# A four-layer graph network on one core: layer 3's gates and layer 1's update computed with features on partitions, and layer 0's identity added to the adjacency in place

## The chip, the core and the metric

The kernel runs on one core of a Trainium2 chip. A core has TensorE (PE: matrix products, and transposes, into PSUM), VectorE (DVE), ScalarE (ACT), GpSimd (POOL) and SyncE (SP, which here issues nearly all DMAs). The metric is the device time of one execution in microseconds (us), lower is better.

## What is computed

There are 32 independent graphs (batches `b`) of 512 nodes with 128 features each, and a dense 512 x 512 adjacency per graph. Everything is float32. Each layer normalises its input `x`, applies a relu, runs a graph layer on it and adds the result to `x`. Cut to what matters:

```python
# layer 0
adj = adj + eye; r = sum(adj, -1) ** -0.5
x = x + leaky_relu((adj * r[:, :, None] * r[:, None, :]) @ (h @ W) + b)
# layer 1
in_rep, out_rep, node_rep = elu(h @ W_in.T + b_in), elu(h @ W_out.T + b_out), elu(h @ W_node.T + b_node)
upd = concat([adj @ in_rep, node_rep, adj.T @ out_rep])
x = x + tanh(upd @ W_upd.T + b_upd)
# layer 2: four sub-layers with l2-normalised adj and adj.T
# layer 3 (a GRU cell)
m = tanh(adj @ (h @ W_msg.T + b_msg))
r = sigmoid(m @ Wih_r + h @ Whh_r + b_r); z = sigmoid(m @ Wih_z + h @ Whh_z + b_z)
n = tanh(m @ Wih_n + bih_n + r * (h @ Whh_n + bhh_n))
x = x + (1 - z) * n + z * h
```

## The kernel before

**Two layouts.** A tile of one graph is 128 partitions x 512 values. In "rows" the nodes lie on partitions (four chunks of 128 nodes, 128 features each); in "features" (names ending in T, and `f`, `agg`, `y` of layer 2) the features lie on partitions and the 512 nodes along the row. The residual `x` and the normalisation live in rows, since the moments of a node are then taken along a partition. Products with the adjacency take rows as the stationary operand and give features. So the stages turn between the layouts. `turned` (L645) does it without PE: a DVE transpose of 32 x 32 blocks into `blk` (L649), four DMAs of 64 KB into a DRAM buffer (L658), one DMA of 256 KB back (L662), and a copy or an addition that reads the result in another order of columns (`turned_cols`). In batches 0, 1 and 31 (`at_ends`) four PE transposes do it instead (L677, L800, L1069).

**The order.** `program(b)` records the operations of each batch with an engine, an estimated cost and what they read and write. `Plan.order` (L173) then runs a list scheduler over all of them: an operation's key is its batch's due time (`PERIOD` per batch, `ENDING` for the last) less the length of the chain behind it, and buffers come from counted pools (`bank` 8 PSUM banks, `s2` tiles of 2 KB per partition, `s4`, `s8` for adjacency). The order that comes out is the static order of each engine's queue. Loads marked `yields` are planned only while no turn is under way (`plan.way`). `kept_warm` (L257) writes filling products (`ps_idle`, L1137) where the plan has PE idle for more than 0.7 us. Two to three batches are in work at a time.

**What the change touches.**
- Layer 0, L923 and after: `diag` gets the four diagonal blocks of `aT` plus the identity (`own`, one DVE addition into a tile of its own). The sum over neighbours then takes for each of four chunks the diagonal block from `diag` and the rest from `aT`, ten products of 128 to 384 columns into `ps_agg`.
- Layer 1's update: `linear_rows` (L696) with the node data as the stationary operand, twelve products of 128 columns that give rows; then the bias `u1` (DVE, L981), tanh (ACT, L983) and the addition to `x1` (DVE, L985).
- Layer 2 starts from `x2`: moments (L586, L588, L589), a power on POOL (L628), `nb` (L636), four ACT operations for `h` (L640), a turn, the copy `f0` (ACT, L682), and the first product `ps_sd<-w_sb,f`.
- Layer 3: `seven("gates", ...)` (L720) computes the 2 x 2 block product of the r and z gates, for nodes in two halves, with seven products instead of eight; each is two products of 128 columns (L759) that give rows. Eight more of 128 columns make the n gate. Biases are added on DVE (`gn`, L1109), then two tanh (L1115), `u`, `n`, `q`, `w`, and `xo` (L1131), which is stored. The last batch goes another way (`gates_turned`, L503).

Of the kernel before, what the change touches and what calls it, by code (L numbers as in the profile page):

```python
# [14 lines left out]
AF = mybir.ActivationFunctionType  # L15
# [9 lines left out]
PERIOD = 35.0  # L25
ENDING = 1.5
SMALL = 8
OWN = 32
# [4 lines left out]
SEVEN = {"last": 0 * 5 * D, "gates": 1 * 5 * D}  # L33
FIFTEEN = 5 * D * len(SEVEN)
# [3 lines left out]
RING = {"inv": 4, "invT": 4}  # L38
# [32 lines left out]
C_COLS = C_L3 + 6  # L71
# [3 lines left out]
R_L0, R_L1_IO, R_L1_UPD, R_L3_MSG, R_L3_G, R_L3_HRZ = (k * D for k in (0, 1, 3, 4, 5, 9))  # L75
R_COLS = 9 * D
# [205 lines left out]
def gnn_stack(  # L282
# [16 lines left out]
    plan = Plan(sb, psum, {"bank": 8, "s2": 39, "s4": 5, "s8": 9}, {"bank": 0, "s2": 5, "s4": 0, "s8": 0})  # L299
# [19 lines left out]
    def t_mm(n):  # L319
        return n * 0.00166 + 0.0085  # L320
# [35 lines left out]
    def blocks(site):  # L356


        if site == "gates":
            return [c + k * D for c in (W_L3_HH, W_L3_IH) for k in range(2)], W3, (r_sb, R_L3_G), (RS, {2})  # L360
        return [W_L2[3][0] + (2 * k + o) * D for k in (2, 0) for o in range(2)], (W2F, {3}), (rf_sb, ROW_OF[3] * 2 * D), RF
# [10 lines left out]
    def setup():  # L372
# [6 lines left out]
        def spread(lo, hi, to=None):  # L379
            return lambda: nc.sync.dma_start(  # L380
                r_sb[:, lo:hi] if to is None else to.ap()[:, :hi - lo], bass.AP(tensor=brow.tensor, offset=brow.offset + lo, ap=[[0, P], [1, hi - lo]]))
# [9 lines left out]
        hrz = plan.buf("s2", (P, N), "hrz")  # L391
        op("SP", 0.5, spread(R_L3_HRZ, R_L3_HRZ + 2 * D, hrz), [], [hrz], kb=D)
        op("DVE", 0.4, lambda: nc.vector.tensor_add(r_sb[:, R_L3_G:R_L3_G + 2 * D], r_sb[:, R_L3_G:R_L3_G + 2 * D], hrz.ap()[:, :2 * D]),
           [(RS, {2}), hrz], [(RS, {2})])
# [50 lines left out]
        for site, at in SEVEN.items():  # L445
            (b11, b12, b21, b22), wbuf, (bias, c), bbuf = blocks(site)
# [11 lines left out]
            combine(4, lambda o, m=bias, c=c: nc.vector.tensor_sub(o, m[:, c:c + D], m[:, c + D:c + 2 * D]), [bbuf])  # L458
# [33 lines left out]
    def program(b):  # L492
# [8 lines left out]
        rows_shape = (P, NC, D)  # L501

# [142 lines left out]
        def turned(m, name):  # L645
# [17 lines left out]
            plan.way(m.uses[0][0], back)  # L663
            return mT

# [54 lines left out]
        def seven(site, x1, x2, dst, part, behind):  # L720

            at = SEVEN[site]
            (b11, b12, b21, b22), wbuf, (bias, bc), bbuf = blocks(site)
# [179 lines left out]
        def tt(dst, fn, n, reads, engine="DVE"):  # L905
            return op(engine, t_tt(n), fn, reads, [dst])

# [12 lines left out]
        def own(k, n):  # L920
            t = aT.ap()
            blocks = bass.AP(tensor=t.tensor, offset=t.offset + k * (N + P), ap=[list(t.ap[0]), [N + P, n], [1, P]])
            own_engine.tensor_tensor(diag.ap()[:, k:k + n, :], blocks, ident[:, None, :].to_broadcast([P, n, P]), op=ALU.add)  # L923

        n = NC if b else 1
        own_engine, own_name = (nc.vector, "DVE") if b < OWN else (nc.gpsimd, "POOL")
        for k in range(0, NC, n):
            op(own_name, t_tt(n * P) if b < OWN else t_pool(n * P), lambda k=k, n=n: own(k, n), [(aT, set(range(k, k + n))), ID], [(diag, set(range(k, k + n)))])
        psh = plan.bank("agg")
        for c in range(NC):  # L930
            for lo, hi in ((0, c * P), (c * P, (c + 1) * P), ((c + 1) * P, N)):
                if lo == hi:
# [3 lines left out]
                   hi - lo, c == 0 and lo == 0, c == NC - 1 and hi == N, [(hr, {c}), (diag if lo == c * P else aT, {c})])  # L936
        agg = buf("s2", name="agg")
# [25 lines left out]
        for h in range(2):  # L963
# [15 lines left out]
        linear_rows(psu, [W_L1_UPD, W_L1_UPD + D, W_L1_UPD + 2 * D], [agg_in, node, agg_out], (W1, {1}))  # L979
        u1, y1 = buf("s2", name="u1"), buf("s2", name="y1")  # L980
        tt(u1, lambda: nc.vector.tensor_add(u1.ap().rearrange("p (c v) -> p c v", c=NC), psu.ap().rearrange("p (c v) -> p c v", c=NC),  # L981
                                            along(r_sb, R_L1_UPD, D, NC)), N, [psu, (RS, {1})])
        op("ACT", t_act(N), lambda: nc.scalar.activation(y1.ap(), u1.ap(), AF.Tanh), [u1], [y1])  # L983
        x2 = buf("s2", rows_shape, "xr")
        tt(x2, lambda: nc.vector.tensor_add(flat(x2), flat(x1), y1.ap()), N, [x1, y1])  # L985
# [43 lines left out]
        for i, (wsd, wn) in enumerate(W_L2):  # L1029
# [8 lines left out]
            if i == 3:  # L1038
                sd = buf("s4", (P, NC, 2 * D), "sd")
                seven("last", f0, f, *of_halves(sd), [third_started])  # L1040
            else:
                sd = paired_rows([f], wsd, (W2F, {i}), rf_sb, RF, ROW_OF[i] * 2 * D)
# [22 lines left out]
        x3 = buf("s2", rows_shape, "xr")  # L1065
        if at_ends:
            pst = plan.bank("t")
            for c in range(NC):
                op("PE", 0.109, lambda c=c: nc.tensor.transpose(pst.ap()[:, c * P:(c + 1) * P], f.ap()[:, c * P:(c + 1) * P], ident),  # L1069
                   [f, ID], [(pst, {c})])  # L1070
            tt(x3, lambda: nc.vector.tensor_add(flat(x3), flat(x2), pst.ap()), N, [x2, pst])
        else:
            f4 = turned(f, "f4r")
# [114 lines left out]
```

## Time and profile before

| what | value |
|---|---|
| median of 4 runs | 2276.22 us (2275.66 to 2276.32) |
| the profiled execution | 2275.91 us, of it 2274.1 in the span of the profile |
| PE matmul instructions | 9328, two for each product, one for each transpose |
| `ps_agg<-a,sd`, 128x512 | x768, 593 ns each by the profile |
| `ps_seven<-t_sb,s`, 128x128 | x756, 275 ns each |
| turns: `turned<-turn_turned`, 256 KB | x116, 2.6 us from issue to landing |
| `turn_turned<-blk`, 64 KB | x464, 1.8 us |
| all DMA queues | q1: 231.29 MB, 32.7% of 16 engines |
| granted PE clock | 1.0 |

A line of a profile's group names the line of the code, the engine, the operation, out<-in by the program's names, shape and count. A wait names who waited and for whom, then the sum in us, how often, and the longest. L353 is the helper through which most products pass, so the names tell more there than the line does.

### The profile page before, as it was taken

What the parts mean: (1) busy time and instruction counts of PE and PEld (TensorE: products, weight loads), DVE (VectorE), ACT (ScalarE), POOL (GpSimd) and SP (SyncE); (2) the same over time, 40 slices, a digit from 0 to 9 for tenths busy, and PEclk for the clock granted to TensorE, in tenths of its full rate; (3) what the DMA queues carried; (4) which work ended last, traced back from release to release, by engine and by line L of the source; (5) the groups of instructions that cost most, each with busy time, mean ns of one, the idle gap of its engine ahead of it and who ended that gap; (6) DMA issues with size and microseconds to landing.
All of it is one profiled execution on the core that took longest, in us unless ns stands there. A gap on an engine that the chain in (4) does not pass through costs nothing.

```text
span 2274.1 us, 28426 instructions
## 1 busy us (share of the span) xinstructions
PE 2267.1 (100%) x9328; PEld 1447.3 (64%) x9328; DVE 1660.8 (73%) x4539; ACT 1016.8 (45%) x2408; POOL 225.9 (10%) x203
## 2 busy tenths in 40 slices
PE   9999999999999999999999999999999999999999
PEld 7666666666566665666666666656666666666666
DVE  7757677777777786777776777767778677777666
ACT  7644344543445533445434455334454344552222
POOL 2100011100011100111000110101110001100000
PEclk9999999999999999999999999999999999999999
DMA  7122333333323333233333333332333323332111
GB/s 281 38 84 76 122 90 107 107 104 121 114 86 107 102 114 119 84 106 102 118 116 94 106 112 98 116 121 81 106 102 116 121 87 111 101 103 77 56 42 51
DMA packets 157444, 233.24 MB, mean 103 GB/s; under 512 B 21360, under 2 KB 96368, under 8 KB 157296
## 3 DMA queue, kind: packets, MB, share of 16 engines
q1 hardware_dynamic: 157008, 231.29, 32.7%
q8 instruction: 74, 1.21, 0.2%
q14 instruction: 74, 0.61, 0.1%
q10 hardware_dynamic: 288, 0.13, 0.0%
HBM read 184.43 MB, written 46.92 MB: 102 GB/s over the span
## 4 chain that ended last, share of the span: by engine, by line
PE 97%; DMA 1%; DVE 1%; ACT 0%; POOL 0%; SPq 0%; issue 0%; ACTq 0%; DVEq 0%
PE ps_agg L353 62%; PE ps_fifteen L838 9%; PE ps_seven L759 9%; PE ps_sd L353 7%; PE ps_upd L353 4%; PE ps_gate L353 3%; PE ps_msg L353 1%; PE ps_lin L353 1%; PE ps_node L353 1%; DMA raw<-in_raw 0%; DMA bounce<-invT 0%; DMA hrz<-in_brow 0%; DMA a<-in_adj 0%; POOL sc L628 0%; DMA turn_turned<-blk 0%; PE ps_t L677 0%
## 5 line engine op out<-in xcount | busy, mean ns | idle before, releaser
L353 PE MATMUL ps_agg<-a,sd 128*128 128x512 f32 x768 | 390.8, 593 | 0.0
L353 PE MATMUL ps_agg<-aT,sd 128*128 128x512 f32 x768 | 372.7, 593 | 0.1
L628 POOL TENSOR_TENSOR sc<-v,neg_half 128x4 f32<-128x4 f32 (+1 forms) x127 | 165.9, 1307 | 1764.7 <-DVE v L589 1165.3
L353 PEld LDWEIGHTS ps_agg<-aT,sd 128*128 128x128 f32 x768 | 137.7, 191 | 104.3 <-issue 98.5
L640 ACT ACTIVATE h<-xr,nb,sc 128x128 f32<-128x128 f32 x384 | 164.3, 485 | 51.6 <-DVE nb L636 50.2
L353 PEld LDWEIGHTS ps_agg<-a,sd 128*128 128x128 f32 x768 | 132.2, 191 | 69.0 <-issue 65.5
L912 ACT ACTIVATE sq<-a 128x512 f32<-128x512 f32 x124 | 78.2, 631 | 202.3 <-DMA a<-in_adj 201.4
L759 PEld LDWEIGHTS ps_seven<-t_sb,s 128*128 128x128 f32 x756 | 111.9, 191 | 46.7 <-issue 37.1
L353 PE MATMUL ps_sd<-w_sb,f 128*128 128x256 f32 x512 | 138.7, 380 | 0.0
L353 PE MATMUL ps_agg<-aT,f1r 128*128 128x512 f32 x256 | 131.0, 593 | 0.1
L353 PE MATMUL ps_agg<-f,w_sb 128*128 128x512 f32 x256 | 130.9, 593 | 0.1
L353 PE MATMUL ps_agg<-aT,rep 128*128 128x512 f32 x256 | 130.7, 593 | 0.1
L353 PE MATMUL ps_agg<-a,rep 128*128 128x512 f32 x256 | 130.7, 592 | 0.0
L353 PE MATMUL ps_agg<-a,f1r 128*128 128x512 f32 x256 | 130.7, 592 | 0.0
L353 PE MATMUL ps_agg<-aT,msg 128*128 128x512 f32 (+1 forms) x264 | 130.0, 580 | 0.0
L353 PEld LDWEIGHTS ps_sd<-w_sb,f 128*128 128x128 f32 x512 | 92.5, 190 | 54.3 <-issue 36.1
L965 ACT ACTIVATE rep<-sd 128x512 f32<-128x512 f32 x64 | 40.1, 628 | 187.4 <-PE ps_agg L353 179.6
L759 PE MATMUL ps_seven<-t_sb,s 128*128 128x128 f32 x756 | 120.0, 275 | 0.0
L1018 DVE TENSOR_TENSOR a<-a,rows 128x512 f32<-128x512 f32 x128 | 87.5, 686 | 42.5 <-PE ps_agg L353 42.1
L715 DVE TENSOR_TENSOR sd<-ps_sd,r_sb 128x512 f32<-128x512 f32 x64 | 44.0, 687 | 98.0 <-PE ps_sd L353 98.0
L715 DVE TENSOR_TENSOR sd<-ps_sd,rf_sb 128x512 f32<-128x512 f32 x128 | 85.8, 671 | 33.3 <-PE ps_sd L353 32.3
L649 DVE STREAM_TRANSPOSE blk<-h 128x512 f32<-128x512 f32 x87 | 61.4, 705 | 60.9 <-ACT h L640 60.9
(224 smaller groups left out, 4673.7 us busy)
## 6 DMA issues: line engine op xcount, KB each, us to landing
aT<-in_adjt SPq DMA_DIRECT2D x124, 512.0 KB, 6.4
a<-in_adj SPq DMA_DIRECT2D x62, 512.0 KB, 5.9
turn_turned<-blk SPq DMA_DIRECT2D x464, 64.0 KB, 1.8
turned<-turn_turned SPq DMA_DIRECT2D x116, 256.0 KB, 2.6
rows<-bounce SPq DMA_DIRECT2D x32, 512.0 KB, 4.0
shares<-bounce SPq DMA_DIRECT2D x32, 512.0 KB, 4.3
x<-in_x SPq DMA_DIRECT2D x32, 256.0 KB, 10.4
out<-xo SPq DMA_DIRECT2D x31, 256.0 KB
```

The lines of the kernel that those rows point to most:

```text
L353: op("PE", t_mm(n), lambda: nc.tensor.matmul(out_of(ps.ap()), lhs(), rhs(), start=start, stop=stop), reads, [ps], later=later)
L628: op("POOL", t_pow(n), lambda: nc.gpsimd.tensor_tensor(inv.ap()[:, :n], v8.ap()[:, :n], neg_half[:, :n], op=ALU.pow), [v8, NH], [(inv, {0})])
L640: op("ACT", t_act(D, 2), lambda c=c: nc.scalar.activation(h.ap()[:, c, :], xin.ap()[:, c, :], AF.Relu, bias=nb.ap()[:, c:c + 1], scale=inv ...
L649: op("DVE", t_tt(N), lambda: nc.vector.transpose(blk.ap().rearrange("p b (c r) -> p c b r", c=NC), m.ap().rearrange("p c (b s) -> p c b s" ...
L715: op("DVE", t_tt(N), lambda ps=ps, h=h: nc.vector.tensor_add(sd.ap()[:, 2 * h:2 * h + 2, :], ps.ap().rearrange("p (j v) -> p j v", j=2), a ...
L759: op("PE", t_mm(D), lambda j=j: nc.tensor.matmul(ps.ap()[:, k * H + j * D:k * H + (j + 1) * D], lhs()[:, j * P:(j + 1) * P], rhs(), start= ...
L838: op("PE", t_mm(H), lambda: nc.tensor.matmul(o[0](), weight(), data[0](), start=first, stop=True, skip_group_check=True), [data[1], wbuf], ...
L912: op("ACT", 0.73, lambda c=c: nc.scalar.activation(sq.ap(), a.ap()[:, c, :], AF.Copy, accum_out=sums.ap()[:, c:c + 1]), [(a, {c})], [sq, ( ...
L965: op("ACT", t_act(N), lambda s=s: nc.scalar.activation(rep.ap()[:, s, :], io.ap()[:, s, :], AF.Exp), [(io, halves)], [(rep, part)])
L1018: op("DVE", t_tt(N), lambda m=m, c=c, s=s: nc.vector.tensor_mul(m.ap()[:, c, :], m.ap()[:, c, :], rows.ap()[:, s, :]), [(m, {c}), rows], [ ...
```

## The change

Layer 3's gates (all batches but the last) are computed with features on partitions: a new function `gates` runs the seven block products with weights as the stationary operand and 256 nodes as moving columns, adds bias and scale in the activations, and gives the cell's output `y` as features. Layer 1's update uses `linear_t` (weights stationary, three products of 512 columns), with the bias in the tanh. Both results are turned back to rows and added to `x` by a new function `added_rows`, which uses `turned`, or PE transposes in batches 0, 1 and 31. In layer 0 (all batches but the first) ACT saves the diagonal blocks of `aT` in `diag`, DVE adds the identity to them in place, four products of 512 columns run over `aT`, and ACT copies the blocks back. The constants of the plan change with it: the cost of a product, `PERIOD`, `ENDING`, the pools, and 16 DRAM buffers for turns instead of 8. The rows of biases for the old gates and the update, with their loads, are gone.

```diff
--- before.py
+++ after.py
-PERIOD = 35.0
-ENDING = 1.5
+PERIOD = 37.0
+ENDING = -3.5
...
-SEVEN = {"last": 0 * 5 * D, "gates": 1 * 5 * D}
-FIFTEEN = 5 * D * len(SEVEN)
+GATES = 5 * D
+FIFTEEN = GATES + 4 * D
...
-RING = {"inv": 4, "invT": 4}
+RING = {"inv": 4, "invT": 4, "turn_turned": 16}
...
-    plan = Plan(sb, psum, {"bank": 8, "s2": 39, "s4": 5, "s8": 9}, {"bank": 0, "s2": 5, "s4": 0, "s8": 0})
+    plan = Plan(sb, psum, {"bank": 8, "s2": 36, "s4": 5, "s8": 10}, {"bank": 0, "s2": 4, "s4": 0, "s8": 0})
...
-        return n * 0.00166 + 0.0085
+        return n * 0.00166 + (0.0123 if n <= P else 0.0094)
...
+        def gates(h3T, mT):
+
+
+            H = N // 2
+            (b11, _, b21, b22), bank = BOTH, {}
+            s12, s34 = (buf("s2", name=k) for k in ("s12", "s34"))
+            hn, r, z, p1, d, n, y, w = (buf("s2", name=k) for k in ("hn", "r", "z", "p1", "d", "n", "y", "w"))
+
+            def half(m, k):
+                return (lambda: m.ap()[:, k * H:(k + 1) * H]), (m, {k})
+
+            def bank_half(name, k):
+                ps = bank[name]
+                return (lambda: ps.ap()[:, k * H:(k + 1) * H]), ps
+
+            def dve(o, x, y, sub=False):
+                op("DVE", t_tt(H), lambda: nc.vector.tensor_tensor(o[0](), x[0](), y[0](), op=ALU.subtract if sub else ALU.add), [x[1], y[1]], [o[1]])
+
+            def product(o, data, weight, wbuf, first):
+                op("PE", t_mm(H), lambda: nc.tensor.matmul(o[0](), weight(), data[0](), start=first, stop=True, skip_group_check=True), [data[1], wbuf], [o[1]])
+
+            def plain(col):
+                return lambda: wt(col), W3
+
+            def made(k):
+                return lambda: t_sb[:, GATES + k * D:GATES + (k + 1) * D], (TS, {GATES + k})
+
+            h0, h1, m0, m1 = half(h3T, 0), half(h3T, 1), half(mT, 0), half(mT, 1)
+            s1, s2, s3, s4 = half(s12, 0), half(s12, 1), half(s34, 0), half(s34, 1)
+            dve(s3, h0, h1, True)
+            bank["n"] = plan.bank("gate")
+            mm(bank["n"], lambda t: t, lambda: wt(W_L3_HH + 2 * D), h3T.ap, N, True, True, [h3T, W3])
+            op("ACT", t_act(N, 1), lambda: nc.scalar.activation(hn.ap(), bank["n"].ap(), AF.Identity, bias=cg_sb[:, 2:3], scale=0.5), [bank["n"], CG], [hn])
+            dve(s1, h1, m1)
+            dve(s2, s1, h0, True)
+            dve(s4, m0, s2, True)
+            for k in "abc":
+                bank[k] = plan.bank("seven")
+            A, Bc, C = bank_half("a", 0), bank_half("b", 0), bank_half("c", 0)
+            P1, D1, E1 = half(p1, 0), half(d, 0), half(d, 1)
+            product(A, h0, *plain(b11), True)
+            op("ACT", t_act(H), lambda: nc.scalar.copy(P1[0](), A[0]()), [A[1]], [P1[1]])
+            product(Bc, s2, *made(1), True)
+            product(C, s1, *made(0), True)
+            dve(D1, Bc, P1)
+            product(A, m0, *plain(b21), False)
+            op("ACT", t_act(H, 1), lambda: nc.scalar.activation(half(r, 0)[0](), A[0](), AF.Tanh, bias=cg_sb[:, 0:1], scale=0.5), [A[1], CG], [(r, {0})])
+            product(Bc, s3, *made(2), False)
+            dve(E1, Bc, P1)
+            dve(half(z, 1), C, E1)
+            product(Bc, m1, *made(3), False)
+            dve(half(r, 1), Bc, P1)
+            op("ACT", t_act(H, 1), lambda: nc.scalar.activation(half(r, 1)[0](), half(r, 1)[0](), AF.Tanh, bias=cg_sb[:, 0:1], scale=0.5), [(r, {1}), CG], [(r, {1})])
+            product(C, s4, *plain(b22), False)
+            dve(half(z, 0), C, D1)
+            op("ACT", t_act(N, 1), lambda: nc.scalar.activation(z.ap(), z.ap(), AF.Tanh, bias=cg_sb[:, 1:2], scale=0.5), [z, CG], [z])
+            bank["i"] = plan.bank("gate")
+            mm(bank["i"], lambda t: t, lambda: wt(W_L3_IH + 2 * D), mT.ap, N, True, True, [mT, W3])
+            tt(hn, lambda: nc.vector.scalar_tensor_tensor(hn.ap(), r.ap(), 1.0, hn.ap(), op0=ALU.add, op1=ALU.mult), N, [r, hn])
+            tt(n, lambda: nc.vector.tensor_add(n.ap(), hn.ap(), bank["i"].ap()), N, [hn, bank["i"]])
+            op("ACT", t_act(N, 1), lambda: nc.scalar.activation(n.ap(), n.ap(), AF.Tanh, bias=cg_sb[:, 3:4]), [n, CG], [n])
+            tt(w, lambda: nc.vector.tensor_sub(w.ap(), h3T.ap(), n.ap()), N, [h3T, n])
+            tt(w, lambda: nc.vector.scalar_tensor_tensor(w.ap(), z.ap(), 1.0, w.ap(), op0=ALU.add, op1=ALU.mult), N, [z, w])
+            tt(y, lambda: nc.vector.scalar_tensor_tensor(y.ap(), w.ap(), 0.5, n.ap(), op0=ALU.mult, op1=ALU.add), N, [w, n])
+            return y
...
-        def turned(m, name):
+        def turned(m, name, quiet=False):
...
-            plan.way(m.uses[0][0], back)
+            if not quiet:
+                plan.way(m.uses[0][0], back)
             return mT
+
+        def added_rows(x, m, quiet=False):
+
+            o = buf("s2", rows_shape, "xr")
+            if at_ends:
+                ps = plan.bank("t")
+                for c in range(NC):
+                    op("PE", 0.109, lambda c=c: nc.tensor.transpose(ps.ap()[:, c * P:(c + 1) * P], m.ap()[:, c * P:(c + 1) * P], ident),
+                       [m, ID], [(ps, {c})])
+                tt(o, lambda: nc.vector.tensor_add(flat(o), ps.ap(), flat(x)), N, [x, ps])
+            else:
+                t = turned(m, "last" if quiet else "turned", quiet)
+                tt(o, lambda: nc.vector.tensor_add(o.ap().rearrange("p c (a r) -> p c a r", a=NC), turned_cols(t), x.ap().rearrange("p c (a r) -> p c a r", a=NC)),
+                   N, [x, t])
+            return o
...
         def own(k, n):
             t = aT.ap()
             blocks = bass.AP(tensor=t.tensor, offset=t.offset + k * (N + P), ap=[list(t.ap[0]), [N + P, n], [1, P]])
-            own_engine.tensor_tensor(diag.ap()[:, k:k + n, :], blocks, ident[:, None, :].to_broadcast([P, n, P]), op=ALU.add)
-
-        n = NC if b else 1
-        own_engine, own_name = (nc.vector, "DVE") if b < OWN else (nc.gpsimd, "POOL")
-        for k in range(0, NC, n):
-            op(own_name, t_tt(n * P) if b < OWN else t_pool(n * P), lambda k=k, n=n: own(k, n), [(aT, set(range(k, k + n))), ID], [(diag, set(range(k, k + n)))])
+            return blocks, ident[:, None, :].to_broadcast([P, n, P])
+
+        def own_blocks():
+            return own(0, NC)[0]
+
+        if b:
+            op("ACT", t_act(N), lambda: nc.scalar.copy(diag.ap(), own_blocks()), [aT], [diag])
+            op("DVE", t_tt(N), lambda: nc.vector.tensor_tensor(own_blocks(), diag.ap(), own(0, NC)[1], op=ALU.add), [diag, ID], [aT])
+        else:
+            for k in range(NC):
+                op("DVE", t_tt(P), lambda k=k: nc.vector.tensor_tensor(diag.ap()[:, k:k + 1, :], *own(k, 1), op=ALU.add), [(aT, {k}), ID], [(diag, {k})])
         psh = plan.bank("agg")
-        for c in range(NC):
+        for c in range(NC if b == 0 else 0):
             for lo, hi in ((0, c * P), (c * P, (c + 1) * P), ((c + 1) * P, N)):
                 if lo == hi:
                     continue
                 mm(psh, lambda t, lo=lo, hi=hi: t[:, lo:hi], lambda c=c: hr.ap()[:, c, :],
                    (lambda c=c: diag.ap()[:, c, :]) if lo == c * P else (lambda c=c, lo=lo, hi=hi: aT.ap()[:, c, lo:hi]),
                    hi - lo, c == 0 and lo == 0, c == NC - 1 and hi == N, [(hr, {c}), (diag if lo == c * P else aT, {c})])
+        if b:
+            aggregate(psh, hr, 0, aT)
+            op("ACT", t_act(N), lambda: nc.scalar.copy(own_blocks(), diag.ap()), [diag], [aT])
         agg = buf("s2", name="agg")
...
-        linear_rows(psu, [W_L1_UPD, W_L1_UPD + D, W_L1_UPD + 2 * D], [agg_in, node, agg_out], (W1, {1}))
-        u1, y1 = buf("s2", name="u1"), buf("s2", name="y1")
-        tt(u1, lambda: nc.vector.tensor_add(u1.ap().rearrange("p (c v) -> p c v", c=NC), psu.ap().rearrange("p (c v) -> p c v", c=NC),
-                                            along(r_sb, R_L1_UPD, D, NC)), N, [psu, (RS, {1})])
-        op("ACT", t_act(N), lambda: nc.scalar.activation(y1.ap(), u1.ap(), AF.Tanh), [u1], [y1])
-        x2 = buf("s2", rows_shape, "xr")
-        tt(x2, lambda: nc.vector.tensor_add(flat(x2), flat(x1), y1.ap()), N, [x1, y1])
+        linear_t(psu, [W_L1_UPD, W_L1_UPD + D, W_L1_UPD + 2 * D], [agg_in, node, agg_out], (W1, {1}))
+        y1 = buf("s2", name="y1")
+        op("ACT", t_act(N, 1), lambda: nc.scalar.activation(y1.ap(), psu.ap(), AF.Tanh, bias=c_sb[:, C_L1_UPD:C_L1_UPD + 1]), [psu, CS], [y1])
+        x2 = added_rows(x1, y1)
...
-        x3 = buf("s2", rows_shape, "xr")
-        if at_ends:
-            pst = plan.bank("t")
-            for c in range(NC):
-                op("PE", 0.109, lambda c=c: nc.tensor.transpose(pst.ap()[:, c * P:(c + 1) * P], f.ap()[:, c * P:(c + 1) * P], ident),
-                   [f, ID], [(pst, {c})])
-            tt(x3, lambda: nc.vector.tensor_add(flat(x3), flat(x2), pst.ap()), N, [x2, pst])
-        else:
-            f4 = turned(f, "f4r")
-            tt(x3, lambda: nc.vector.tensor_add(
-                x3.ap().rearrange("p c (a r) -> p c a r", a=NC), x2.ap().rearrange("p c (a r) -> p c a r", a=NC), turned_cols(f4)),
-               N, [x2, f4])
+        x3 = added_rows(x2, f)
...
-        seven("gates", h3T, mT, lambda k, o: g.ap()[:, 2 * k:2 * k + 2, o * D:(o + 1) * D],
-              lambda k, o: (g, fields((2 * k, 2 * k + 1), (o,))), [messages])
...
-        u, n, q, w, xo = (buf("s2", rows_shape, k) for k in ("u", "n", "q", "w", "xo"))
-        tt(u, lambda: nc.vector.scalar_tensor_tensor(u.ap(), gate(0), 1.0, gate(3), op0=ALU.add, op1=ALU.mult), N, [column(0), column(3)])
-        tt(u, lambda: nc.vector.scalar_tensor_tensor(u.ap(), u.ap(), 0.5, gate(2), op0=ALU.mult, op1=ALU.add), N, [u, column(2)])
-        op("ACT", t_act(N), lambda: nc.scalar.activation(n.ap(), u.ap(), AF.Tanh), [u], [n])
-
-        tt(q, lambda: nc.vector.scalar_tensor_tensor(q.ap(), gate(1), 1.0, h3.ap(), op0=ALU.add, op1=ALU.mult), N, [column(1), h3])
-        tt(w, lambda: nc.vector.scalar_tensor_tensor(w.ap(), gate(1), -1.0, n.ap(), op0=ALU.add, op1=ALU.mult), N, [column(1), n])
-        tt(q, lambda: nc.vector.tensor_sub(q.ap(), q.ap(), w.ap()), N, [q, w])
-        tt(xo, lambda: nc.vector.scalar_tensor_tensor(xo.ap(), q.ap(), 0.5, x3.ap(), op0=ALU.mult, op1=ALU.add), N, [q, x3])
+        new = gates(h3T, mT)
+        xo = added_rows(x3, new, True)
         op("SP", 0.4, lambda: nc.sync.dma_start(out[b], xo.ap()), [xo], [], kb=256, yields=True)
```

## The prediction, made before the changed kernel had run

> **What bounds the kernel now.** I read the page first, then the waits of TensorE (PE), then the chain of waits, then the timeline. Page, PE's waits and the chain:
>
> ```profile
> span 2274.1 us, 28426 instructions
> PE 2267.1 (100%) x9328; PEld 1447.3 (64%) x9328; DVE 1660.8 (73%) x4539; ACT 1016.8 (45%) x2408; POOL 225.9 (10%) x203
> PE 97%; DMA 1%; DVE 1%; ACT 0%; POOL 0%; SPq 0%; issue 0%; ACTq 0%; DVEq 0%
> PE ps_idle L1137 <- POOL ident masks.py:199: 1.4, 1, 1.4
> PE ps_lin L353 <- ACT agg L938: 0.9, 1, 0.9
> PE ps_t L677 <- ACT h L640: 0.4, 1, 0.4
> PE ps_msg L353 <- ACT hT L679: 0.2, 1, 0.2
> ```
>
> The reader is to see that PE waited four times in the whole run, 2.9 us together, and never in the steady loop: three are at the start and one is in the last batch. So the time is the sum of the distances between PE's instructions. The next thing needed is that distance, start to start, by shape. These are timeline lines (start, length, engine, line, instruction); every product is two instructions (x2), a transpose one:
>
> ```profile
> 36.79 0.38 PE L353 MATMUL ps_agg<-diag,h 128*128 128x128 f32 x2
> 37.01 0.81 PE L353 MATMUL ps_agg<-aT,h 128*128 128x384 f32 x2
> 37.66 0.38 PE L353 MATMUL ps_upd<-w_sb,agg_in 128*128 128x128 f32 x2
> ...
> 40.34 0.39 PE L353 MATMUL ps_agg<-aT,h 128*128 128x128 f32 x2
> ...
> 42.96 1.28 PE L1137 MATMUL ps_idle<-ident 128*128 128x128 f32 x10
> ...
> 55.90 0.60 PE L677 MATMUL ps_t<-ident,h 128*128 128x128 f32 x4
> 56.34 1.88 PE L353 MATMUL ps_agg<-aT,sd 128*128 128x512 f32 x4
> ...
> 61.49 1.89 PE L353 MATMUL ps_sd<-w_sb,hT 128*128 128x256 f32 x8
> 63.22 0.60 PE L800 MATMUL ps_t<-ident,f 128*128 128x128 f32 x4
> ...
> 1101.96 1.02 PE L353 MATMUL ps_agg<-aT,f1r 128*128 128x512 f32 x2
> ...
> 1111.40 1.02 PE L353 MATMUL ps_agg<-a,rep 128*128 128x512 f32 x2
> ```
>
> From them: twelve 128-column products 37.66 to 40.34, 0.2233 us each; four of 256 columns 61.49 to 63.22, 0.4325; eleven of 512 columns 1101.96 to 1111.40, 0.858; four transposes 55.90 to 56.34, 0.11. Layer 0's ten pieces took 0.87 (36.79 to 37.66) and 2.62 (40.34 to 42.96), 3.49 together. The lengths (0.38 for what takes 0.22) overlap and can't be summed.
>
> **What the Trainium skill says.** "Perfetto Trace Analysis", section Tensor Engine Instruction: the profiler estimates a matmul's end rather than observing it. The trace agrees (1.02 long, 0.858 apart), so I use starts. "TensorE: Matmul & The Clock Gate", Back-to-back issue gap: the isolated gap is a part proportional to the columns plus a small constant. The trace agrees in form: four 128-column products take 0.893, one of 512 columns 0.858, so fewer and longer instructions save 0.035 per 512 columns. "DMA: Bandwidth & Descriptors", Anatomy of one DMA, gives some 2.0 us of fixed cost per DMA; here 64 KB took 1.8 and 256 KB 2.6 us to land. The same page, Two DMAs through the same engine are not ordered: the issuer must wait for the first before it issues one that reads its data. The trace shows that hold on SP's queue (below).
>
> **The change part by part, in PE time.** The columns of the removed and the added products are equal; only their number changes. The order of the changed kernel, from its instruction list, gives the counts.
> - Gates, 31 batches. Removed: 14 products of L759 and 8 of the n gates, 22 x 0.2233 = 4.913. Added: 7 of 256 columns and 2 of 512, 3.028 + 1.716 = 4.744. Saved 0.169 x 31 = 5.2 us.
> - Layer 1's update, 32 batches: 2.68 against 3 x 0.858 = 2.574. Saved 0.106 x 32 = 3.4.
> - Layer 0's sum, 31 batches: 3.49 against 4 x 0.858 = 3.432. Saved 0.058 x 31 = 1.8.
> - Turning back in the batches that use PE for it (0, 1, 31): 12 transposes for layer 1, 8 for the gates, 20 x 0.11 = 2.2 lost. Elsewhere the turning is a DVE transpose and five DMAs.
> - Filling products (ps_idle), written where the plan sees over 0.7 us of idle PE: 56 before, 63 now, none of them between the start and the last batches in either. 7 x 0.2233 = 1.6 lost.
>
> Sum on PE: -10.4 + 2.2 + 1.6 = -6.6 us.
>
> The other engines. DVE per batch loses about 13.2 us (twelve 256-element operations at 0.41, four of `ev`, `dv` and `gn` at 0.68, six of the gate's end at 0.69, two of the update at 0.68) and gets about 10.0 (nine at 0.42, five at 0.69, two transposes at 0.71, the two additions 0.69): some 95 us less over the run. ACT gains about 2.8 us per batch (two copies of the diagonal at 0.6, the gates' biases), 90 us, to about 49%. Both cost nothing while PE is busy beside them. SP issues ten more DMAs for each of 29 batches (two turns, 2 x (1.76 + 0.34) us of its queue); the DMA engines' 33% would rise by about 30 MB in 233. The additions to the diagonal happen in place, so the sums and squares of `aT` (L991, L994) can't start until the copy back; they were done long before their readers, so I take nothing.
>
> The end: the order puts batch 30's last addition (it waits for a DMA turn) before DVE's last two additions, and its 256 KB store before the last half store on SP. Before, DVE's last addition ended at 2271.5 and the span at 2274.1. Bounds: 0 if the turn landed early, 2.6 (what 256 KB takes to land) if the store is wholly in the way; I take +1.2. The start: the waits of 0.9 and 0.4 us stand in a stretch that is reordered; bounds 0 to -1.3, I take -0.6.
>
> Total -6.0. The profiled execution took 2275.91 (span 2274.1 and 1.8 around it), so 2269.9; the runs' median lies 0.3 above it, so 2270.2; I say 2270.
>
> **The one new wait that matters.** The path from layer 1's update to layer 2's first product gets a second DMA turn. Before:
>
> ```profile
> 1120.10 0.39 PE L353 MATMUL ps_upd<-w_sb,agg_out 128*128 128x128 f32 x2
> ...
> 1130.57 1.75 SPq L658 DMA_DIRECT2D turn_turned<-blk  x4
> 1133.72 0.34 SPq L662 DMA_DIRECT2D turned<-turn_turned  x1
> ...
> 1137.01 0.60 ACT L682 COPY f<-turned 128x512 f32<-128x512 f32 x1
> ...
> 1138.28 1.03 PE L353 MATMUL ps_sd<-w_sb,f 128*128 128x256 f32 x4
> ```
>
> The update ended at 1120.32, `f0` was ready at 1137.61, PE took it at 1138.28: 0.67 us to spare. SP issued the read-back 3.15 us after the first write, and what is behind it on SP stands still meanwhile. The bare durations (u 0.69, y 0.63, addition 0.67, moments 1.46, power 1.0, nb 0.15, four h 1.7, transpose 0.7, turn 6.5, copy 0.6, drain 0.16) sum to 14.3, so 3.0 us were queueing. In the new order the products between the update's last and `f0`'s first sum, by the distances above, to 22.9 us (18.0 before). The bare path becomes 0.16 + 0.69 + 0.71 + 6.5 + 0.69 + 1.46 + 1.0 + 0.15 + 1.7 + 0.7 + 6.5 + 0.6 = 20.9. That leaves 2.0 us for queueing where 3.0 were used. And the update's turn stands on SP behind the read-back of batch b-2's `h3`, whose write may land 0.5 to 1 us after the update's block is ready. So the wait here is between nothing and about 0.7 us per batch (3.0 - 2.0, less the 0.3 us that one operation fewer, `u`, queues for), times 29. I take nothing, because the turns before were ready ahead of PE (`f1r` by 0.44, `hT` by 0.66, `f0` by 0.67), but this is the weak step.
>
> **Rivals.**
> - *Small wait*: 0.05 to 0.35 us per batch at `ps_sd<-w_sb,f` gives most of it back; at 0.15, 29 x 0.15 = 4.4, so 2274.5. For: the count above. Against: before has no such wait at any of five turns per batch.
> - *Slower*: the same place, the update's turn held on SP behind the read-back and under running loads of `a` and `aT`; at 0.5 us per batch +14.5, so 2284.5. It decides from (6.0 + 4.6) / 29 = 0.37 us. For: one turn before took 6.9 instead of 6.5. Against: loads give way to open turns, and DVE has 3 us per batch less to do.
> - *More gained*: end and start cost nothing: 2270 - 1.2 - 1.6 - 0.7 = 2266.5. For: DVE lighter. Against: the filling products are in the order.
> - That the change doesn't do what it says is excluded by the counts: 4694 products, transposes and fillings before, 3844 now.
>
> **How the numbers follow.** Forecast 0.54, small wait 0.24, slower 0.14, more gained 0.08. The forecast's own range is 2267.5 to 2272.5 (end 0 to 2.6, start 0 to -1.3, distances by 1 us). To hold 8 in 10: 2266 to 2281, which takes in the small wait and the edge of the slower case. 0.2% of 2276.2 is 4.6 us (what a measurement here can tell from none): faster is under 2271.6. Faster: 0.9 of the forecast, all of the larger gain and 0.05 of the small waits: 0.58. Slower 0.14, same 0.28.
>
> **What would show it.** Right: about 7600 matmul records ((3844 - 80) x 2 + 80, transposes counted once), no waits of PE in the loop, the loop's pattern repeating after 69.4 us instead of 69.7 (in the chain of waits, 1101.26 to 1170.97), `ps_upd` a row of 128x512 at 593 ns. Wrong: a wait of `ps_sd` on ACT `f` some 29 times, or of any product on a turn; a span end more than 4 us after the last product.

## The result, and the profile after

The changed kernel took 2272.02 us (median of 31 runs, 2269.53 to 2275.66), the kernel before 2276.24 us (49 runs, 2275.27 to 2277.38): a ratio of 0.9983, interval 0.9978 to 0.9988. The gain is 4.2 us where 6.2 were forecast. The profiled execution took 2272.94 us, span 2271.1; before, 2275.91 and 2274.1. From the page of the changed kernel (span; busy time of the engines; shares of the chain that ended last), and then from its view of PE's waits (engine, line waited for, total us, times, longest):

```profile
span 2271.1 us, 25755 instructions
PE 2261.7 (100%) x7608; PEld 1311.8 (58%) x7608; DVE 1605.4 (71%) x4346; ACT 1101.5 (48%) x2563; POOL 218.1 (10%) x203
PE 93%; DVE 3%; DMA 2%; ACT 1%; SPq 0%; issue 0%; POOL 0%; ACTq 0%; DVEq 0%; POOLq 0%
```

```profile
PE ps_agg L353 <- DVE rep L1049: 2.0, 4, 0.9
PE ps_idle L1170 <- POOL ident masks.py:199: 1.4, 1, 1.4
PE ps_agg L353 <- ACT h L673: 1.1, 2, 0.6
PE ps_sd L353 <- ACT hT L755: 0.2, 1, 0.2
```

The reader is to see two things. PE has 7608 records instead of 9328, as counted. And PE's share of the chain fell from 97% to 93%, though PE is as busy as before: at a wait the chain leaves PE for all the work that led to it, some 15 us each at three of the waits in the first line of the second fence. The kernel before doesn't have them: the products of layer 1's sum wait for `rep`, four times.

To see where the time went I took, from both traces, the distance of each PE start to the next, less the usual distance of its shape. What is over by more than 0.06 us counts as a wait, and the rest is the sum of distances:

| part of the span, us | before | after | difference | forecast |
|---|---|---|---|---|
| distances | 2259.4 | 2252.5 | -6.9 | -6.6 |
| waits in the loop (70 to 2150) | 1.3 | 4.2 | +2.9 | 0 |
| waits at the start | 6.9 | 7.3 | +0.4 | -0.6 |
| waits at the end, and after the last product | 5.2 | 5.9 | +0.7 | +1.2 |
| sum | | | -3.0 | -6.0 |

The distances gave what was counted; the waits in the loop gave 2.9 us of it back. The sum is -3.0 and not the -4.2 of the medians because it compares two single executions: that of the changed kernel lay 0.9 us above its median, that of before 0.3 below. How much the loop's waits are in other executions isn't known.

Where that comes from is shown by the chain of waits of the changed kernel at one of these waits (start, us, what):

```profile
600.75 0.70 DVE y L560
601.47 0.72 DVE blk L709
...
603.57 0.43 SPq L718
604.00 0.05 issue
604.05 0.02 SPq L639
604.07 0.03 issue
604.10 4.86 DMA x<-in_x
608.96 0.02 issue
608.98 0.87 DVE bn L646 x4
609.85 0.28 DVE mv L648 x4
610.13 0.57 DVE sd L791
...
612.37 0.61 DVE rep L1049
612.98 0.14 issue
613.12 7.22 PE ps_agg L353 x16
```

Read from below: PE waits for `rep`, `rep` stands on DVE behind `sd`, `sd` behind `bn`, and `bn` waits for the load of `x`. But this `x` is that of a later batch: nothing in `rep` needs it. DVE stood idle for 2.1 us before `bn` and took `sd` only after it, though the products that `sd` reads had ended at 607.96: its queue goes in order, so an operation without haste, whose data is late, holds one that PE needs. `x` is late because SP issued its load (L639) only after the four writes of the gates' new turn (L718), and these waited for `y`, the gates' result.

This place of `x` is the same in batches 7 to 31. In the changed kernel `x` is issued 2.8 us (their median) before `bn` starts; in the kernel before, some 12 us. It usually lands just in time. Three times it took 4.3 to 4.9 us to `bn`, and these three are followed by three of the four waits for `rep`, 1.9 us of PE (1.03 at 613.12, 0.48 at 1030.18, 0.40 at 1377.64). With the short gaps between the products right behind each wait they cost 2.4 us.

The fourth wait for `rep`, 0.7 us (0.9 with its gaps), has another cause. It is that of batch 31, when all loads of `x` have long landed (the last was issued at 1994.5):

```profile
2139.08 0.69 DVE L738 TENSOR_TENSOR xr<-last,xr 128x512 f32<-128x512 f32 x1 [2.47 <-DMA last<-turn_last]
2139.69 0.68 DVE L791 TENSOR_TENSOR sd<-ps_sd,r_sb 128x512 f32<-128x512 f32 x1
2141.74 0.69 DVE L1049 TENSOR_TENSOR rep<-rep,sd 128x512 f32<-128x512 f32 x1
2142.57 1.10 PE L353 MATMUL ps_agg<-aT,rep 128*128 128x512 f32 x2 [0.55 <-DVE rep L1049]
```

Here `sd` and `rep` stand on DVE behind `xr`, the addition of the gates' own new turn, which waited 2.5 us for the turn's read-back. This is read from the trace; no run moved that addition. The waits at other places in the loop are 0.8 us, against 1.3 before.

### The profile page after: what moved, and what is told of

Read it like the earlier page. It is cut to its first block, busy times and chain, and to the rows that moved or that the text cites. A ratio compares the mean times of both kernels' runs of the same rounds, so it can differ in the third digit from the quotient of the medians.

```text
span 2271.1 us, 25755 instructions
## 1 busy us (share of the span) xinstructions
PE 2261.7 (100%) x7608; PEld 1311.8 (58%) x7608; DVE 1605.4 (71%) x4346; ACT 1101.5 (48%) x2563; POOL 218.1 (10%) x203
## 4 chain that ended last, share of the span: by engine, by line
PE 93%; DVE 3%; DMA 2%; ACT 1%; SPq 0%; issue 0%; POOL 0%; ACTq 0%; DVEq 0%; POOLq 0%
PE ps_agg L353 59%; PE ps_fifteen L914 9%; PE ps_sd L353 7%; PE ps_seven L835 4%; PE ps_seven L516 4%; PE ps_upd L353 3%; PE ps_gate L353 3%; PE ps_msg L353 1%; PE ps_lin L353 1%; PE ps_node L353 1%; DMA x<-in_x 1%; DMA turned<-turn_turned 0%; SPq L718 0%; DMA turn_turned<-blk 0%; DMA bounce<-invT 0%; ACT h L700 0%
## 5 line engine op out<-in xcount | busy, mean ns | idle before, releaser
L353 PE MATMUL ps_agg<-aT,sd 128*128 128x512 f32 x768 | 380.2, 593 | 0.0
L688 POOL TENSOR_TENSOR sc<-v,neg_half 128x4 f32<-128x4 f32 (+1 forms) x127 | 152.2, 1198 | 1706.3 <-DVE v L649 1599.6
L353 PE MATMUL ps_sd<-w_sb,f 128*128 128x256 f32 x512 | 145.3, 379 | 0.0
L1136 ACT ACTIVATE f<-c,cf_sb 128x512 f32<-128x512 f32 x64 | 46.2, 722 | 178.6 <-DVE c L1135 178.6
L353 PE MATMUL ps_agg<-aT,h 128*128 128x512 f32 (+2 forms) x260 | 128.7, 583 | 0.5 <-ACT h L673 0.5
L353 PE MATMUL ps_agg<-aT,rep 128*128 128x512 f32 x256 | 121.6, 595 | 2.0 <-DVE rep L1049 2.0
L353 PE MATMUL ps_agg<-aT,msg 128*128 128x512 f32 (+1 forms) x264 | 116.7, 579 | 0.0
L1096 DVE TENSOR_TENSOR a<-a,rows 128x512 f32<-128x512 f32 x128 | 87.1, 685 | 16.5 <-PE ps_agg L353 15.9
L1077 POOL TENSOR_TENSOR inv<-stat,neg_half 128x8 f32<-128x8 f32 x32 | 59.5, 1859 | 308.7 <-DVE stat L1076 300.2
L1096 DVE TENSOR_TENSOR aT<-aT,rows 128x512 f32<-128x512 f32 x128 | 86.2, 682 | 1.8 <-DMA rows<-bounce 1.8
L1136 ACT ACTIVATE f<-ps_agg,cf_sb 128x512 f32<-128x512 f32 x32 | 22.0, 687 | 131.9 <-PE ps_agg L353 131.9
```

The source lines that it names most:

```text
L353: op("PE", t_mm(n), lambda: nc.tensor.matmul(out_of(ps.ap()), lhs(), rhs(), start=start, stop=stop), reads, [ps], later=later)
L688: op("POOL", t_pow(n), lambda: nc.gpsimd.tensor_tensor(inv.ap()[:, :n], v8.ap()[:, :n], neg_half[:, :n], op=ALU.pow), [v8, NH], [(inv, {0})])
L1077: roots = op("POOL", t_pow(2 * NC) + 0.4, lambda: nc.gpsimd.tensor_tensor(inv.ap()[:, :2 * NC], stat.ap(), neg_half, op=ALU.pow), [stat, N ...
L1096: op("DVE", t_tt(N), lambda m=m, c=c, s=s: nc.vector.tensor_mul(m.ap()[:, c, :], m.ap()[:, c, :], rows.ap()[:, s, :]), [(m, {c}), rows], [ ...
L1136: end = op("ACT", t_act(N, 1), lambda to=to, i=i, f_new=f_new: nc.scalar.activation(f_new.ap(), to.ap(), AF.Tanh, bias=cf_sb[:, i:i + 1]), ...
```

## Experiments

The theory after this reading (X): `x`'s place behind the gates' turn costs the loop its waits. Rivals: the new turn of layer 1's update makes PE wait (T), or the traffic of the added turns makes landings late at random, wherever they stand (C).

**x's load early.** SP issues it right after the read-back ahead of the gates' turn; nothing else is moved by hand:

```diff
-        plan.kept_warm(plan.order(), idle_products, 1.3)
+        done = plan.order()
+        for b in range(7, B):
+            at = next(i for i, o in enumerate(done) if o.engine == "SP" and o.bufs[-1].name == f"x_{b}")
+            to = max(i for i in range(at) if done[i].engine == "SP" and done[i].bufs[-1].name.startswith("turned_"))
+            done.insert(to + 1, done.pop(at))
+        plan.kept_warm(done, idle_products, 1.3)
```

> One edit to the changed kernel: in SP's queue the load of x of batches 7 to 31 stands before the four writes of turn_last instead of behind them; nothing else moves. Theory X (the changed kernel's new waits come from VectorE, which stands at the moments of a later batch's x until that load has landed, and so gives layer 1's rep late to TensorE): the load is issued some 10 us earlier, VectorE's bn no longer waits on x in the loop, no ps_agg waits for rep, the loop's waits fall from about 4 us to under 1, median 2269.5 to 2270, runs within about 2 us. Theory T (the prediction's: the second turn on the way from layer 1's update to layer 2): nothing changes, 2272, runs spread over 6 us. Theory C (the added turns' traffic makes landings late at random, wherever they stand): waits move to other landings, 2271 to 2273.

Measured: 2269.95 us (10 runs, 2268.87 to 2272.2), ratio to the kernel before 0.9974 (0.9964 to 0.9983). SP's timeline, first of the changed kernel and then of this one:

```profile
593.22 0.34 SPq L722 DMA_DIRECT2D turned<-turn_turned  x1
602.21 1.79 SPq L718 DMA_DIRECT2D turn_last<-blk  x4
604.10 0.39 SPq L639 DMA_DIRECT2D x<-in_x  x1
```

```profile
591.75 0.34 SPq L722 DMA_DIRECT2D turned<-turn_turned  x1
592.19 0.37 SPq L639 DMA_DIRECT2D x<-in_x  x1
600.72 1.78 SPq L718 DMA_DIRECT2D turn_last<-blk  x4
```

SP stood idle for 8.6 us between the read-back (593.22 and its 0.34) and the writes (602.21); that is where the load could have gone. No wait for `rep` is left, and the waits in the loop fall from 4.2 to 2.2 us, where under 1 was expected. All four waits for `rep` with their gaps, 3.3 us, are gone, and waits at other places have grown from 0.8 to 2.2. So X holds for the three that followed a late `x`, and the net gain is smaller than what they cost. The fourth is gone without an edit aimed at it: at the same place `xr` waited 1.5 us instead of 2.5.

**x's load late.** The opposite: after the read-back of the gates' turn. The diff is the same but for the place, `to = min(... startswith("last_"))`.

> The opposite edit: the load of x stands behind the read-back of turn_last, about 1.75 us later (604.10 against 605.85 in the profile of the changed kernel). X: bn waits about 1.8 us in each of 25 batches; the three waits in the profile gave TensorE 1.03, 0.48 and 0.40 us for 2.14, 1.59 and 1.51 us of waiting, so what VectorE waits over 1.1 us comes through: about 0.7 us per batch, 25 x 0.7 = 17, median 2286 to 2292. T and C: unchanged, 2271 to 2274.

Measured: 2308.71 us (4 runs, 2308.38 to 2309.01), ratio 1.0142 (1.0128 to 1.0156). PE's waits, and then the one line of DVE's waits that answers to them:

```profile
PE ps_agg L353 <- DVE rep L1049: 20.2, 24, 2.2
PE ps_msg L353 <- ACT hT L758: 3.3, 6, 0.7
```

```profile
DVE bn L646 <- DMA x<-in_x: 57.3, 27, 3.8
```

The wait for `rep` is now there in 24 batches, so the sign and the place are X's. The size was missed by a factor of two: waits in the loop came to 38 us, where 17 were expected. The cover between `bn` and PE was as the expectation took it: DVE waits 2.1 us per batch on average and PE 1.0 after it, 1.1 less. What it had too small is DVE's wait (1.8), and what it left out are the short gaps behind these waits, 6 us, and new waits at other products, 7 us.

**The buffers of before.** The pools' sizes alone, on the changed kernel:

```diff
-    plan = Plan(sb, psum, {"bank": 8, "s2": 36, "s4": 5, "s8": 10}, {"bank": 0, "s2": 4, "s4": 0, "s8": 0})
+    plan = Plan(sb, psum, {"bank": 8, "s2": 39, "s4": 5, "s8": 9}, {"bank": 0, "s2": 5, "s4": 0, "s8": 0})
```

> The changed kernel with the pools of before (39 s2 tiles, 9 s8, 5 kept). The plan puts the load of x beside those of the adjacency, well before its use. X: no waits on x in the loop, 2269.5 to 2270.5, small spread. T and C: 2271 to 2273. If the tenth adjacency tile is what keeps the loads away from the turns, other waits appear and it is slower than the changed kernel.

Measured: 2269.46 us (7 runs, 2268.59 to 2272.33), ratio 0.9972 (0.9962 to 0.9983). `x` is issued about 7.5 us before its use, and PE has no wait for `rep`. So the late `x` came out of the plan with the pool sizes of the change; the turn on SP isn't enough by itself. Which of the three sizes does it was not tried. The profiled run was the slowest of the seven (2272.33) and has 4.1 us of waits in the loop, at other places.

**Both together:** the early load and these pools.

> The kernel with x's load early and with the pool sizes of before (s2 39, s8 9). If both edits cure the one wait for x, they don't add: 2269.5, loop excess 1.5 to 2.5 us, no wait of ps_agg on rep. If each cures another wait, or the scatter of some 3 us from run to run comes from scarce buffers: 2268.0, and a scatter under 2 us.

Measured: 2269.59 us (7 runs, 2268.2 to 2272.41), ratio 0.9973 (0.9962 to 0.9984). They don't add, as two cures of one wait wouldn't; with these pools the edit moves the load only ahead of a store and two loads (9.0 instead of 7.5 us before its use). Waits in the loop are 0.6 us, less than expected, but 8.0 us stand at the start. The scatter of 4 us from run to run stays: its cause isn't settled.

**The update's turn taken away** (theory T). On the kernel with the early load, `x2 = added_rows(x1, y1, on_pe=True)` with `if at_ends or on_pe:`, so that PE turns the update back in every batch.

> x_early, with layer 1's update turned back to rows by four TensorE transposes in every batch, so that the path from the update to layer 2 has one DMA turn as before the change. Distances: 116 transposes more x 0.11 = 12.8 us, and 10 more filling products (73 against 63) x 0.22 = 2.2, so x_early + 15 us, about 2285, if the update's turn costs TensorE nothing. T: the turn's waits go, so 2 to 3 us less than that.

Measured: 2290.49 us (4 runs, 2289.05 to 2291.7), ratio 1.0062 (1.0048 to 1.0076). The transposes cost the 15 us of distance (14.9 from the trace), and waits in the loop rise from 2.2 to 7.5 us rather than vanish. That is not what T says, but this edit gives another order as well, so the run can't settle it alone. The trace of the changed kernel can: no product there waits for `f0`, the copy behind the update's turn, so T isn't the cause of its waits. (With the pools of before one product does, for 0.5 us.) The timeline of the changed kernel shows the place that the prediction worried about:

```profile
1115.19 1.02 PE L353 MATMUL ps_upd<-agg_out,w_sb 128*128 128x512 f32 x2
...
1117.82 1.74 SPq L718 DMA_DIRECT2D turn_turned<-blk  x4
1120.96 0.34 SPq L722 DMA_DIRECT2D turned<-turn_turned  x1
...
1124.55 0.68 DVE L738 TENSOR_TENSOR xr<-turned,xr 128x512 f32<-128x512 f32 x1
...
1131.35 1.79 SPq L718 DMA_DIRECT2D turn_turned<-blk  x4
1134.54 0.34 SPq L722 DMA_DIRECT2D turned<-turn_turned  x1
...
1137.28 0.62 ACT L758 COPY f<-turned 128x512 f32<-128x512 f32 x1 [1.04 <-DMA turned<-turn_turned]
...
1138.91 0.59 PE L353 MATMUL ps_sd<-w_sb,f 128*128 128x256 f32 x2
```

From the end of the update's products (1115.19 + 0.86) to the first use of `f0` are 22.9 us; the path took 21.8, and `f0` was ready 1.0 us ahead, where it was 0.67 before.

**The plan's two numbers.** The changed kernel with `PERIOD = 35.0` and `ENDING = 1.5`.

> The changed kernel with the plan's PERIOD 35 and ENDING 1.5 of before; x is not moved. 90 filling products in the order instead of 63, all at the start and in the last batches. Theory (the two constants count only by the fillings): 27 x 0.2233 = 6.0 us more, 2278.0, with the loop's waits for rep still there (2 to 3 us). Rival (the constants shift x's load in SP's queue, so the late x is their doing): the loop's waits go and 2275 remains.

Measured: 2278.64 us (21 runs, 2276.72 to 2280.45), ratio 1.0012 (1.0005 to 1.0018). Distances +6.0, waits in the loop 4.2 as in the changed kernel, but only one of them, 0.3 us, is for `rep`. The theory is right in its sum and wrong in its place: the waits went elsewhere. The rival is wrong in its sum, since other waits took the place of those for `rep`, but right in its mechanism: `x` is now issued 5.3 us before its use instead of 2.8, and DVE waits for it once in batches 7 to 31 (1.6 us). So the old pools or the old numbers alone each give `x` a longer lead; the late `x` takes the change's pools and numbers together.

**One part undone.** Layer 0 in ten pieces again, on the kernel with the early load:

```diff
-            op("ACT", t_act(N), lambda: nc.scalar.copy(diag.ap(), own_blocks()), [aT], [diag])
-            op("DVE", t_tt(N), lambda: nc.vector.tensor_tensor(own_blocks(), diag.ap(), own(0, NC)[1], op=ALU.add), [diag, ID], [aT])
+            op("DVE", t_tt(N), lambda: nc.vector.tensor_tensor(diag.ap(), *own(0, NC), op=ALU.add), [aT, ID], [diag])
...
-        for c in range(NC if b == 0 else 0):
+        for c in range(NC):
...
-        if b:
-            aggregate(psh, hr, 0, aT)
-            op("ACT", t_act(N), lambda: nc.scalar.copy(own_blocks(), diag.ap()), [diag], [aT])
```

> The kernel with x's load early, with layer 0's identity in a tile of its own and the sum in ten pieces again, as before the change; the rest is the changed kernel. Theory (the pieces cost PE what the distances say, the copies cost nothing): 31 x 0.058 = 1.8 us more of PE distance and one filling product less (-0.2), so 2269.95 + 1.6 = 2271.5. Rival (the addition in place holds aT until the copy back, and the two ACT copies stand ahead of other work): without them the waits left in the loop, 2 us, go too, and the time is 2269.5. In the timeline the ten pieces must take 3.49 us again against 3.43 of the four products.

And layer 1's update by rows again, with its row of biases, on the same kernel:

```diff
-        linear_t(psu, [W_L1_UPD, W_L1_UPD + D, W_L1_UPD + 2 * D], [agg_in, node, agg_out], (W1, {1}))
...
-        x2 = added_rows(x1, y1)
+        linear_rows(psu, [W_L1_UPD, W_L1_UPD + D, W_L1_UPD + 2 * D], [agg_in, node, agg_out], (W1, {1}))
...
+        tt(x2, lambda: nc.vector.tensor_add(flat(x2), flat(x1), y1.ap()), N, [x1, y1])
```

> The kernel with x's load early, with layer 1's update by rows again (twelve products of 128 columns, the bias added by DVE, no turn back). Theory (PE's distances alone): 32 x 0.106 = 3.4 more, 8 filling products more than before (+1.8), 12 transposes fewer (-1.3): 2269.95 + 3.9 = 2273.9. Rival (the update's turn is what still makes PE wait in the loop and at the start): its removal gives back some 2 of the 2.05 us of excess in the loop, so 2271.9.

Measured: layer 0 undone 2282.54 us (5 runs, 2281.59 to 2286.96), ratio 1.0032 (1.002 to 1.0045); layer 1 undone 2279.17 (21 runs, 2276.58 to 2281.92), ratio 1.0015 (1.0008 to 1.0021). Both sums missed by far, 11 and 5 us, and both rivals too. The distances against the kernel with the early load are right: +1.8 for 1.6 expected, +4.0 for 3.9. The waits are not: in the loop 12.7 and 4.2 us instead of 2.2, and with layer 1 undone 8.2 instead of 5.7 at the start. The largest of the first, in its chain of waits:

```profile
982.27 5.09 DMA turned<-turn_turned
987.36 0.02 issue
987.38 0.62 ACT hT L758
988.00 0.28 ACT pb L911
988.28 0.04 issue
988.33 0.70 PE ps_fifteen L914 x2
```

It is the same pattern on another engine: `pb`, which PE waits for, stands on ACT behind `hT`, a copy that waits for a turn.

**One part alone**, on the kernel before, with its own plan numbers and pools: layer 0's diff, layer 1's, and the gates' (the diff of the change, each part by itself).

> The kernel before with layer 0's part of the change alone (identity added in place, sum in four products), the plan's numbers and pools as before. Its order has 72 filling products, 16 more than before. Theory (PE's distances and fillings are all there is): -1.8 + 16 x 0.2233 = +1.8, so 2278.0. Rival (in this order some operation of ACT or DVE comes late, as in the run that undid this part): 5 to 10 us of waits of PE in the loop, 2283 or more.

> The kernel before with layer 1's part alone (features on partitions, turned back by DMA), the plan's numbers and pools as before; 60 filling products, 4 more. Theory: -3.4 + 0.9 + 12 x 0.11 = -1.2, so 2275.0, and no wait of ps_sd on f. Rival (the second turn in the path to layer 2's first product has no cover when the rest of the kernel is as before): 0.15 to 0.5 us in each of 29 batches at ps_sd<-f, 2279 to 2289.

> The kernel before with the gates' part alone (features on partitions, turned back by DMA), the plan's numbers and pools as before; 82 filling products, 26 more. Theory: -5.2 + 26 x 0.2233 + 8 x 0.11 = +1.5, so 2277.7, with x issued 10 us or more ahead of its use, since the pools are those of before. Rival (the four writes of turn_last hold x's load on SP whatever the pools): x issued about 3 us ahead, 2 to 3 us of waits of ps_agg on rep more, 2280.5.

And the kernel before with the plan's numbers of the change (`PERIOD = 37.0`, `ENDING = -3.5`, the price of a product) and nothing else:

> The kernel before with the changed kernel's PERIOD 37, ENDING -3.5 and price of a product, and nothing else of the change. 89 filling products, 33 more than before. Theory (the plan's numbers count by the fillings alone): 33 x 0.2233 = +7.4, so 2283.5, with no waits of PE in the loop. Rival (each set of numbers gives another order on every engine, and the order decides whether PE waits): 10 us or more of waits in the loop beside the fillings, 2293 or more.

The theory missed the time of all four by 11 to 18 us, though its distances were right within 2. The rivals of layer 0 alone and of the new plan numbers, waits from another order, hold, though layer 0's had 5 to 10 us of them:

| kernel | median, us (runs) | ratio, interval | distances against before: expected, measured | waits in the loop |
|---|---|---|---|---|
| layer 0 alone | 2289.47 (4) | 1.006, 1.0045 to 1.0075 | +1.8, +2.2 | 11.6 |
| layer 1 alone | 2293.31 (4) | 1.0068, 1.0051 to 1.0085 | -1.2, +0.7 | 23.3 |
| gates alone | 2294.08 (4) | 1.008, 1.0065 to 1.0095 | +1.5, +1.2 | 12.8 |
| before, new plan numbers | 2300.78 (4) | 1.0104, 1.0087 to 1.0121 | +7.4, +8.1 | 16.5 |

Layer 1 alone scattered from 2287.5 to 2302.1, and its profiled run was the longest of the four, so its waits are an upper case. PE's waits there:

```profile
PE ps_agg L354 <- DVE diag L938: 5.0, 6, 1.7
PE ps_msg L354 <- ACT hT L697: 3.0, 4, 1.7
PE ps_fifteen L853 <- DVE yx L847: 1.6, 3, 1.0
...
PE ps_sd L354 <- ACT f L697: 1.1, 1, 1.1
```

Only one of them is at `ps_sd<-f`, where the rival had put 29. In the gates alone `x` is issued some 6.4 us ahead, between what the two sides expected, and no wait is for `rep`.

So no part makes the kernel faster by itself in the order that it gets with the old numbers, and the new numbers do the old kernel no good. Each edit gives another order on all engines, and the orders differ by 1 to 23 us of waits in the loop. The two orders of the comparison, before (1.3) and after (4.2), are among those that wait little. This is not C as it was put. The early load keeps the added traffic and loses the waits for `rep`, and the median landing hardly changed from before to after (256 KB from 2.6 to 2.7 us, 64 KB 1.8 in both). Whether the traffic has a part in single late landings is not shown. That a given order waits is shown; which property of an order makes it so, beyond the chains above, is open.

## Why the prediction was right, and where it was not

- *The bound.* "So the time is the sum of the distances between PE's instructions": right. Distances by shape, with the counts of products and fillings, gave -6.6, and -6.9 were measured; those of the experiments, from -7.0 to +8.1, were met within 0.7 us, but for one that missed by 1.9. The single parts (gates -5.2, update -3.4, layer 0 -1.8) are borne out for layer 0 and the update by the two undone kernels, for the gates by the kernel with them alone. One reading was too clean: the four waits of the view leave out short ones, and by distances the loop of before has 1.3 us of them.
- *The loop's waits: the term that failed.* The prediction took nothing, and gave as the weak step the path of `f0` over two turns. That path was worked out well: 22.9 us forecast and found, bare 20.9 and 21.8 with its queueing, and PE finds `f0` ready. The queueing used 0.9 us of the 2.0 left to it. The missing 2.9 us came in through another sentence: "SP issues ten more DMAs for each of 29 batches (two turns, 2 x (1.76 + 0.34) us of its queue)". It priced the new instructions by their own time on SP and didn't ask what stands behind them while they wait for `y`. It knew the hold ("what is behind it on SP stands still meanwhile") but followed it only to `f0`. Behind the gates' turn stood `x`, behind `x` on DVE stood `sd` and `rep`, and behind these PE: 2.4 us by the trace, with the sign confirmed by the early and the late load. The turn's own addition on DVE did the same once more, 0.9 us, by the trace alone. Other waits were 0.5 less than before.
- *The start.* Taken as -0.6, it was +0.4; in the kernel with the early load, whose order there is the same, it is 1.2 us less than before. One profile can't tell these apart.
- *The end.* Taken as +1.2 with bounds 0 and 2.6, it was +0.7. The mechanism is the one forecast. In the chain of waits of the changed kernel, batch 30's last addition stands between DVE's last ones:

```profile
2267.10 0.19 DVE xo L617
2267.30 0.60 DVE xr L738
2267.90 0.20 DVE xo L617
```

- *The other engines.* The lengths of DVE's instructions sum to 98 us less, where 95 were counted; its busy time, in which what overlaps counts once, fell by only 55. ACT's busy time rose by 85, where 90 were counted. Neither set the time by its sum; DVE did by its order.
- *The rivals.* "Small wait" was the closest in size (2.9 us given back; it priced 4.4) and wrong in place. The slower one's place had no wait at all. Of the signs of being right, the 7608 records and the pattern of 69.4 us (334.50 to 403.87 in the chain) came, "no waits of PE in the loop" did not.
- *Luck.* The median, 2272.02, lies in the forecast's own range, 2267.5 to 2272.5. But that range was made of the end, the start and the distances, with no wait in the loop, so that it holds the result is in part luck. The line it drew for "faster", under 2271.6, was missed by 0.4 us.

## What to carry to other kernels

Where an instruction is added that waits for data, list what stands behind it on its queue and follow each to the engine that sets the time: the price is not its own length, and the victim may belong to another batch. An early load of an input that needs nothing is worth more ahead of such an instruction than behind it; here that move lowered the median by 2.1 us (2269.95; 2269.46 with the pools of before, which can't be told from it; both intervals just overlap that of the change). Where a planner makes the order, an edit changes the sum of work, which could be counted here, and the waits, which the counts did not give; compare parts by distances and waits apart, and don't add up times of single parts.

## What the hardware showed that was not expected

The three late landings of `x` in the changed kernel have something in common. Two windows of its DMA view, the first with a late `x` (603.5 to 609.5), the second with one in time (533 to 538); columns are queue, packets, MB and share of 16 engines:

```profile
q1 hardware_dynamic: 801, 1.05, 65.3%
q8 instruction: 1, 0.02, 1.5%
```

```profile
q1 hardware_dynamic: 785, 0.66, 59.0%
```

In the first a fetch of instructions, one packet of 16 KB, runs beside the load; it took 1.4 us (1.5% of 16 engines for 6 us). The same is so in all three. In the changed kernel and the one with the late `x` I found 33 loads in the loop whose landing DVE waited for. Of the 22 without such a fetch between issue and use none took longer than 3.4 us; of the 11 with one, five did, 3.9 to 4.9. That is an association, not a shown cause: nothing here moved a fetch to see `x` follow. If the fetch is the cause, a load that is timed to land just before its use is what it would hurt.

The other is the scatter: 2 us from run to run before, 6 us after, 3.3 with the early load. But these are 49, 31 and 10 runs, and the kernel with the late `x` spread by only 0.6 us in 4. So whether the short lead of `x` has a part in it is not shown; the cause stays open.
